# A four-layer image kernel: the column-wise copy of an image made by transfers in memory, after layer 0's merge, in place of copies on ScalarE during it

## The chip, the cores and the metric

The kernel runs on one core of a Trainium2 chip. The metric is the device time in microseconds (us). A run's time is a little longer than the span of its profile, which begins with the first recorded instruction and ends with the last. The engines are named as the profile names them: PE (TensorE), DVE (VectorE), ACT (ScalarE), POOL (GpSimd) and SP (SyncE, which here only issues transfers). All data is float32.

## What is computed

The input is two images of 128 channels and 128 x 128 pixels. Four layers follow each other, each of the form x + layer(groupnorm(x)): an axial attention along the columns (layer 0), a chain of four directional scans (layer 1), a deformable 3 x 3 convolution (layer 2), and a 4 x 4 convolution with stride 2 in transformed form (layer 3). The change lies between layers 0 and 1. Cut to what matters, layer 1 is:

```python
def _pass_once(x, w, vertical, reverse):
    if not vertical:
        x = jnp.transpose(x, (0, 1, 3, 2))
    if reverse:
        x = jnp.flip(x, axis=2)
    xs = jnp.moveaxis(x, 2, 0)
    def step(carry, xi):
        y = xi + jax.nn.relu(_conv1d(carry, w))      # 9 taps, 128 channels to 128
        return (y, y)
    _, ys = lax.scan(step, xs[0], xs[1:])
    ...
x = _pass_once(x, w_ud, vertical=True, reverse=False)
x = _pass_once(x, w_du, vertical=True, reverse=True)
x = _pass_once(x, w_lr, vertical=False, reverse=False)
x = _pass_once(x, w_rl, vertical=False, reverse=True)
...
x = x + _L1_conv_ref(_gn(x), ...)                    # the x that is added is layer 0's output
```

So the image that leaves layer 0 is needed twice: normalised, as the input of the scans, and untouched, to be added to their result. Two scans go through the rows and two through the columns; the last goes through the columns from right to left.

## The kernel before

**The tile `both`.** One tile of 128 partitions (channels) by 2 images by 128 rows by 128 columns, 128 KB in each partition, holds both images from the merge to the end (`res[n]` is image n). The four scans work in it in place, so layer 0's output is gone from it once layer 1 has normalised and scanned it.

**Layer 0** leaves its two parts in memory: `sv`, by column, and `sve`, by row. `Merge` (L889) puts them together in 16 half units: a unit is 32 columns of one image, a half unit 16. Units 0 to 3 are image 0, units 4 to 7 image 1. For each half unit `run` (L968) does this:

- `add` (L987), twice with 8 columns: ACT scales 8 columns of the sums `tv` into a tile `u` (L992), turning them to row order; DVE scales the part `te` and adds `u` to it (L1001). `u` has two buffers.
- `to_image` (L1003): POOL adds the upper 64 rows of `te` to the image, DVE the lower 64 (L1010); then DVE takes four pieces of group statistics, the lower rows first, so that the last two wait for POOL (L1012).
- `by_column` (L1016), one half unit late: ACT copies 8 columns of the finished image to a tile `bc` in column order and issues its store to the scratch tensor `x1_d` in memory, twice (L1021, L1023). `x1_d` is thus stored by column. `bc` has three buffers.

The loads of `te` (2 MB a unit), `tv` (1 MB a half unit) and the input image (1 MB for 16 rows) are issued on SP in a written order (`InOrder`, which also holds the order of the engines' instructions): a `te` two units ahead, a `tv` one unit ahead. `te` and `tv` have two buffers each, so a load waits until the buffer's last reader is done. All transfers of SP and ACT share eight semaphores in turn; one waits for the transfer before it on its semaphore, about eight back.

**Layer 1** (L1064) begins with the group norm's coefficients `gs` and `gb` (L1075), loads three more sets of scan weights on ACT's queue (L1058; POOL makes sums of them, L1060), and calls `layer3_weights` (L1694): it loads layer 3's weights `ta` on ACT's queue (L1706), POOL makes the transformed weights of it in 25 small instructions (L1713 to L1743), and the result `w3w` is stored to memory, again on ACT's queue (L1745), for layer 3 to read much later. Then come the scans.

A line of a scan is one row (or column) of both images. Its 9 taps are done in three groups of products with the even and odd pixels apart: 14 matmuls of 128 x 128 by 128 or 130 columns on PE (L1158). ACT copies the first product out as `c0` (L1168), DVE makes `v`, `u` and the new even and odd halves `new[0]`, `new[1]` and their sum `new[2]` (L1169 to L1175). These feed the next line's products, so a scan is one chain of dependent lines. In scans 0 to 2 ACT writes the new line back into `both` with two copies, `res<-ln` in the profile (L1178). In scan 0 ACT also normalises the rows in place, four ahead (L1105, L1128). The last scan doesn't write back by copy: POOL adds the new line and the saved column of layer 0's output into `both` (L1181). Those columns come from `x1_d` in blocks `x1t` of 8 columns (1 MB, three buffers), loaded on SP two blocks ahead (L1095, L1135).

Layer 2 and layer 3 follow; the change doesn't touch them except for where layer 3's weights come from in time.

Of the kernel before, what the change touches and what calls it, by code (L numbers as in the profile page):

```python
# [7 lines left out]
F32 = mybir.dt.float32  # L8
# [7 lines left out]
P = 128  # L16
N = 2
S = 128
RT = 4
NT = S // RT  # L20
WC = 32
# [867 lines left out]
class Merge:  # L889

    def __init__(self, env, x, mem, x1_d, ctx):
        self.env, self.x, self.mem, self.x1_d, self.ctx = env, x, mem, x1_d, ctx
        self.units = [(n, wc) for n in range(N) for wc in range(NC)]
        self.sums, self.embedded = {}, {}
        self.sync = InOrder(env.tc, env.nc.sync)
# [69 lines left out]
    def run(self, prm, res, mv, st_gn):  # L968
        nc, tc = self.env.nc, self.env.tc
        HWC, HS = WC // 2, S // 2  # L970
        act, dve, pool = (InOrder(tc, e) for e in (nc.scalar, nc.vector, nc.gpsimd))
        sp, units = self.sp, self.units
        with ExitStack() as ctx:
            cp = ctx.enter_context(tc.tile_pool(name="mg_c", bufs=1))
            pp = ctx.enter_context(tc.tile_pool(name="mg_ps", bufs=1, space=PSUM))
            for part in range(4):
                self.load_rows(res[0], 0, part)
            a, shift = self.scales(cp, pp, prm, mv)

            def there(at, hf):  # L980
                n, wc = units[at]
                lo = wc * WC + hf * HWC
                return res[n][:, :, lo : lo + HWC]

            HQ = HWC // 2

            def add(at, hf):  # L987

                tv = self.sums.pop((at, hf))
                for q in range(2):  # L990
                    u = sp.tile([P, S, HQ], F32, name="u", tag="u")
                    act.activation(  # L992
                        u.rearrange("p h w -> p w h"),
                        tv[:, q * HQ : (q + 1) * HQ],
                        AF.Identity,
                        bias=shift,
                        scale=a[:, 0:1],
                    )
                    lo = hf * HWC + q * HQ
                    te = self.embedded[at][:, :, lo : lo + HQ]  # L1000
                    dve.scalar_tensor_tensor(te, te, a[:, 1:2], u, ALU.mult, ALU.add)  # L1001

            def to_image(at, hf):  # L1003

                n, wc = units[at]
                te = self.embedded[at][:, :, hf * HWC : (hf + 1) * HWC]
                image = there(at, hf)
                for h, engine in ((0, pool), (HS, dve)):
                    here = image[:, h : h + HS, :]
                    engine.tensor_tensor(here, te[:, h : h + HS, :], here, ALU.add)  # L1010
                for b in (2, 3, 0, 1):
                    dve.bn_stats(  # L1012
                        st_gn[:, n, wc * NB + hf * 4 + b, :], image[:, b * 32 : (b + 1) * 32, :]
                    )

            def by_column(at, hf):  # L1016
                n, wc = units[at]
                image = there(at, hf)
                for q in range(2):
                    t = sp.tile([P, HQ, S], F32, name="bc", tag="bc", bufs=3)  # L1020
                    act.copy(t, image[:, :, q * HQ : (q + 1) * HQ].rearrange("p h w -> p w h"))  # L1021
                    lo = wc * WC + hf * HWC + q * HQ
                    act.dma_start(out=self.x1_d[:, n, lo : lo + HQ, :], in_=t)  # L1023

            last = None
            for at in range(len(units)):
                for hf in range(2):
                    if at > 0:  # L1030
                        add(at, hf)
                        if at + 1 < len(units):
                            self.load_sums(at + 1, hf)
                    elif hf == 0:
                        for k in range(2):
                            add(0, k)
                            self.load_sums(1, k)
                        self.load_rows(res[1], 1, 0)
                        self.load_rows(res[1], 1, 1)
                    if last is not None:  # L1040
                        by_column(*last)
                    last = at, hf
                    to_image(at, hf)
                if at + 2 < len(units):
                    self.load_embedded(at + 2)
                if at in (0, 1):
                    self.load_rows(res[1], 1, at + 2)
            by_column(*last)

# [9 lines left out]
    return wl, ws  # L1061


def layer1(env, prm, res, both, x1_d, st_gn, st_next, first, prepare):  # L1064

# [1 line left out]
    nc, tc = env.nc, env.tc  # L1069
    HS = S // 2  # L1070
    with ExitStack() as ctx:
        cp = ctx.enter_context(tc.tile_pool(name="l1c", bufs=1))
        sp = ctx.enter_context(tc.tile_pool(name="l1s", bufs=3))
        with tc.tile_pool(name="l1pn", bufs=1, space=PSUM) as pn:
# [1 line left out]
        pp = ctx.enter_context(tc.tile_pool(name="l1ps", bufs=2, space=PSUM))  # L1076
        weights = [first] + [scan_weights(env, prm, cp, d) for d in range(1, 4)]
        prepare()
        xp = ctx.enter_context(tc.tile_pool(name="l1x", bufs=3))


        lines = [
# [7 lines left out]
            InOrder(tc, e) for e in (nc.tensor, nc.vector, nc.scalar, nc.gpsimd)  # L1090
        )

        CB = 8

        def load_columns(w0):  # L1095
            t = xp.tile([P, N, CB, S], F32, name="x1t", tag="x1t")
            nc.sync.dma_start(out=t, in_=x1_d[:, :, w0 : w0 + CB, :])
            return t

        def stats(t, n):  # L1100
# [17 lines left out]
        for d in range(4):  # L1118
            steps = list(range(S)) if d % 2 == 0 else list(range(S - 1, -1, -1))
            wl, ws = weights[d]  # L1120
            if d == 3:
                columns = {w0: load_columns(w0) for w0 in (S - CB, S - 2 * CB)}
            for at, line in enumerate(steps):
# [7 lines left out]
                new = [t[:, :, 2 : 2 + HS] for t in now]  # L1131
                if d == 3:
                    w0 = line // CB * CB
                    if line == w0 + CB - 1 and w0 >= 2 * CB:
                        columns[w0 - 2 * CB] = load_columns(w0 - 2 * CB)  # L1135
                    add = [columns[w0][:, :, line - w0, k::2] for k in range(2)]
                if at == 0:
                    for k in range(2):
                        dve.tensor_copy(new[k], here[k])
# [554 lines left out]
def layer3_weights(env, prm, w3_d):  # L1694
# [5 lines left out]
    with tc.tile_pool(name="l3w", bufs=1) as wp:  # L1700
# [2 lines left out]
        tk = [wp.tile([P, 4, 2, H], F32, name=f"tk{k}", tag=f"tk{k}") for k in range(2)]  # L1703
        w3 = wp.tile([P, W3], F32, name="w3w", tag="w3w")
        ws, wt = layer3_views(w3)
        nc.scalar.dma_start(out=ta.rearrange("p u v o -> p (u v o)"), in_=prm["w3"])  # L1706
        pool = nc.gpsimd
        zero = wp.tile([P, 2 * P], F32, name="zero", tag="zero")
        pool.memset(zero, 0.0)
# [27 lines left out]
        for half in range(2):  # L1737
# [4 lines left out]
            if half == 1:  # L1742
                pool.tensor_tensor(to[2], y, x, sub)  # L1743
                less(to[3], x, y)
        nc.scalar.dma_start(out=w3_d, in_=w3)  # L1745


def layer3(env, prm, res, w3_d, st_gn, out):
# [173 lines left out]
@with_exitstack  # L1922
def program(ctx, tc, prm, out):
    nc = tc.nc
    x = prm["x"]
    cst = ctx.enter_context(tc.tile_pool(name="cst", bufs=1))
    dram = ctx.enter_context(tc.tile_pool(name="scratch", bufs=1, space=DRAM))
    env = Env(tc, cst, prm["cst"])
    st_gn = [
        cst.tile([P, N, NT, 6], F32, name=f"st_gn{k}", tag=f"st_gn{k}") for k in range(2)  # L1930
    ]
    mem = {
        "qa": dram.tile([P, N, NC, WC, S], F32, name="qa_d", tag="qa_d"),
        "qb": dram.tile([P, N, NC, 4, 4, 8, WC], F32, name="qb_d", tag="qb_d"),
        "v": dram.tile([NG, N, NC, S, WC, 16], F32, name="v_d", tag="v_d"),
        "sv": dram.tile([P, N, NC, WC, S], F32, name="sv_d", tag="sv_d"),
        "sve": dram.tile([P, N, NC, S, WC], F32, name="sve_d", tag="sve_d"),
    }
    w3_d = dram.tile([P, W3], F32, name="w3_d", tag="w3_d")
    x1_d = dram.tile([P, N, S, S], F32, name="x1_d", tag="x1_d")  # L1940
    mem["px"] = dram.tile([N, TP, TP, P], F32, name="px_d", tag="px_d")
    mem["off"] = dram.tile([N, NT, P, 4, 27], F32, name="off_d", tag="off_d")
    tables = [
        dram.tile([TE * TE, 512], F32, name=f"table{n}", tag=f"table{n}") for n in range(N)
    ]

    alphas = cst.tile([P, NG, 3], F32, name="alphas", tag="alphas")
    layer0_prepare(env, x, prm, mem, alphas)
    mv = cst.tile([P, NG, 2, 2], F32, name="mv_out", tag="mv_out")
    merging = ctx.enter_context(ExitStack())  # L1950
    merge = Merge(env, x, mem, x1_d, merging)
    layer0_attention(env, prm, mem, alphas, mv, merge.begin)

    rp = ctx.enter_context(tc.tile_pool(name="res", bufs=1))
    both = rp.tile([P, N, S, S], F32, name="res", tag="res")
    res = [both[:, n] for n in range(N)]
    with tc.tile_pool(name="l1w", bufs=1) as wp:
        first = scan_weights(env, prm, wp, 0)
        merge.run(prm, res, mv, st_gn[1])
        merging.close()  # L1960
        layer1(
            env,
            prm,
            res,
            both,
            x1_d,
            st_gn[1],
            st_gn[0],
            first,
            lambda: layer3_weights(env, prm, w3_d),  # L1970
        )
    layer2(env, prm, res, mem, tables, st_gn[0], st_gn[1])
    layer3(env, prm, res, w3_d, st_gn[1], out)
# [129 lines left out]
```

## Time and profile before

| what | value |
|---|---|
| three runs | 5618.76, 5618.18, 5607.35 us; median 5618.18 |
| the profiled execution: its own time | 5624.39 us |
| its span | 5622.6 us |
| mean granted clock of PE in it | 0.966 |
| PE busy, share of the span | 5229.8 us, 93% |
| DVE, ACT, POOL busy | 66%, 47%, 27% |
| first load of the merge's image issued | 1966.5 us |
| last statistics of the merge end | 2129.6 us |
| first scan's first product, about | 2166 us |
| POOL's first add of the fourth scan | 3376.9 us |
| transfers: bytes, mean rate | 404.21 MB, 72 GB/s |

How to read it. The profile's second part cuts the span into 40 slices of 140.6 us; a digit is the busy share of an engine in tenths. In the view of stretches, each engine has its busy time in the stretch and the number of its instructions; then follow the clock granted to PE, the mean busy share of the 16 DMA engines and what they moved. In the view of waits, a line says who waited for whom: total us, how often, longest. In the timeline each row is a start, a duration and an instruction, out<-in with shapes; what stands in brackets is the idle time before it and what ended it. Nearly all of this kernel's instructions carry line 81, since the helper `InOrder` issues them; one goes by the names of tiles. `pl` is a scan's product in PSUM, `ln` the line's halves, `res` the image in `both`, `x_d` the scratch tensor `x1_d`.

### The profile page before, as it was taken

Reading aid. Unit: us, or ns where it says so; the run is one execution under the profiler, and the core shown is the slowest. Engines: PE = TensorE matmul, PEld = TensorE weight load, DVE = VectorE, ACT = ScalarE, POOL = GpSimd, SP = SyncE. Lnnn points to the kernel's source line nnn. Section 1 sums busy time; section 2 is a strip of 40 time slices with the busy share of each in tenths; the row PEclk is TensorE's granted clock in tenths of the full one; section 3 lists DMA queues with packets and bytes.
Section 4 is the critical chain, followed back from the end, with each engine's and each line's share of the span. In section 5 each row is a group of like instructions: output and inputs, shape, how many; then the busy total and the mean of one; then the engine's idle time right before and its main releaser. Section 6 shows DMA issues by size and latency. Waiting matters only on the chain. (4 is left out here: it accounts for less than half of the span.)

```text
span 5622.6 us, 171669 instructions
## 1 busy us (share of the span) xinstructions
PE 5229.8 (93%) x71931; PEld 4656.8 (83%) x71931; DVE 3685.4 (66%) x7132; ACT 2652.3 (47%) x7896; POOL 1530.1 (27%) x1169
## 2 busy tenths in 40 slices
PE   8997999999999805999999999999799999999999
PEld 6866888888888605999999999994599998999877
DVE  3635888888888764555555556663466666666698
ACT  1056899898898774443223330003233333333322
POOL 2114666666666632000000003330000000000376
PEclk8998999999999957999999999999899999999999
DMA  3353333333333392000000001104567677766211
GB/s 151 107 219 84 60 60 61 62 62 61 60 61 60 94 396 89 1 1 2 1 1 1 1 1 39 39 25 121 105 88 88 88 83 85 91 88 87 47 50 57
DMA packets 413991, 404.21 MB, mean 72 GB/s; under 512 B 63520, under 2 KB 368544, under 8 KB 402336
## 3 DMA queue, kind: packets, MB, share of 16 engines
q1 hardware_dynamic: 404000, 365.18, 31.7%
q10 hardware_dynamic: 9216, 27.95, 1.3%
q8 instruction: 576, 9.44, 0.7%
q14 instruction: 199, 1.63, 0.1%
HBM read 252.31 MB, written 140.68 MB: 70 GB/s over the span
## 5 line engine op out<-in xcount | busy, mean ns | idle before, releaser
L81 PE MATMUL pl<-ln,wl 128*128 128x128 f32 (+1 forms) x10160 | 1239.6, 276 | 31.4 <-DVE ln L81 31.4
L81 PEld LDWEIGHTS pl<-ln,wl 128*128 128x128 f32 x10160 | 1176.3, 190 | 42.3 <-issue 28.0
L81 ACT ACTIVATE e<-e,mx 128x128 f32<-128x128 f32 x2048 | 798.4, 398 | 0.8 <-DVE mx L81 0.8
L81 ACT COPY sm<-ps_s 128x432 f32<-128x432 f32 (+1 forms) x768 | 319.0, 489 | 787.3 <-PE ps_s L81 787.3
L81 POOL TENSOR_TENSOR e<-e,total 128x1024 f32<-128x1024 f32 x256 | 485.6, 1897 | 477.6 <-DVE total L81 466.6
L81 ACT COPY res<-ln 128x128 f32<-128x128 f32 x762 | 263.3, 345 | 721.3 <-DVE ln L81 721.3
L81 PE MATMUL ps_s<-s,xw 100*128 100x144 f32 x4096 | 545.0, 286 | 0.1
L81 POOL TENSOR_TENSOR res<-ln,x1t 128x128 f32<-128x128 f32 x256 | 134.1, 524 | 1495.3 <-DVE ln L81 1495.3
L81 DVE COPY s<-ps_w 100x1152 f32<-100x1152 f32 x256 | 346.6, 1354 | 294.1 <-PE ps_w L81 293.9
L81 PE MATMUL po<-sm,wdef 128*128 128x256 f32 x2304 | 539.1, 379 | 0.0
L81 PE MATMUL pl<-ln,ws 128*128 128x128 f32 x4064 | 537.5, 274 | 0.0
L81 POOL COPY et<-et 128x1024 f32<-128x1024 f32 x256 | 516.4, 2017 | 33.1 <-DVE et L81 24.5
L81 PEld LDWEIGHTS ps_s<-s,xw 100*128 100x128 f32 x4096 | 517.0, 190 | 0.6 <-ACT sm L81 0.5
L81 DVE TENSOR_TENSOR v<-pl,c 128x128 f32<-128x128 f32 x508 | 148.2, 292 | 538.2 <-PE pl L81 538.2
L81 PEld LDWEIGHTS pl<-ln,ws 128*128 128x128 f32 x4064 | 495.3, 191 | 0.0
L81 ACT ACTIVATE r<-gen,alphas 128x1536 f32<-128x1536 f32 x256 | 395.4, 1544 | 169.2 <-PE gen L81 138.6
L81 PEld LDWEIGHTS po<-sm,wdef 128*128 128x128 f32 x2304 | 419.8, 190 | 47.7
L81 POOL MEMSET col<- 128x10 f32 (+1 forms) x72 | 6.0, 123 | 1483.2 <-DVE res L81 1475.6
L81 ACT ACTIVATION_READ_ACCUMULATOR e<-e,mx 128x1 f32 x2048 | 400.0, 195 | 0.0
L81 DVE SCALAR_TENSOR_TENSOR ln<-v,res 128x128 f32<-128x128 f32 x1016 | 343.7, 338 | 49.2 <-DVE v L81 1.2
L81 PE MATMUL te<-cst_main,e 128*128 128x128 f32 x2048 | 337.8, 287 | 27.1 <-POOL e L81 20.1
L81 DVE COPY et<-te 128x512 f32<-128x512 f32 x512 | 349.2, 682 | 13.4 <-PE te L81 12.6
(245 smaller groups left out, 9215.3 us busy)
## 6 DMA issues: line engine op xcount, KB each, us to landing
xw<-px_d SPq DMA_DIRECT2D x1280, 80.0 KB
xa<-in_x SPq DMA_DIRECT2D x16, 1024.0 KB
v_d<-vs SPq DMA_DIRECT2D x16, 1024.0 KB
qb_d<-sb SPq DMA_DIRECT2D x16, 1024.0 KB
qa_d<-sa SPq DMA_DIRECT2D x8, 2048.0 KB
zz<-qb_d SPq DMA_DIRECT2D x1024, 16.0 KB
vt<-v_d SPq DMA_DIRECT2D x64, 256.0 KB
qk<-qa_d SPq DMA_DIRECT2D x256, 64.0 KB
```

The lines of the kernel that those rows point to most:

```text
L81: return lambda *a, **k: self.tc.keep_in_program_order(issue(*a, **k))
```

## The change

It has four parts. By-column copies and their stores go from the merge (`by_column` and its calls), and `u` gets four buffers. At the start of layer 1, 17 transfers on SP store `both` to `x1_d` by row: rows 0 to 3, then 15 blocks of 8 rows, then rows 124 to 127. After `prepare()`, eight transfers on SP copy `x1_d` to a second scratch tensor `x1c_d` from memory to memory, the last block of columns first; `x1c_d` holds blocks of 16 columns, in each of which a partition's part is contiguous. One such transfer moves 32768 runs of 64 bytes, 2 MB. The fourth scan loads blocks of 16 columns (2 MB, two buffers, one block ahead), in which a column's elements lie 64 bytes apart. And `layer3_weights` issues its load and its store on SP in place of ACT. In the built program the load of `ta` stands behind the 17 row stores on SP, and the store of `w3w` behind the first of the eight copies and ahead of the other seven.

```diff
@@ Merge.run
-                    u = sp.tile([P, S, HQ], F32, name="u", tag="u")
+                    u = sp.tile([P, S, HQ], F32, name="u", tag="u", bufs=4)
...
-            def by_column(at, hf):
-                n, wc = units[at]
-                image = there(at, hf)
-                for q in range(2):
-                    t = sp.tile([P, HQ, S], F32, name="bc", tag="bc", bufs=3)
-                    act.copy(t, image[:, :, q * HQ : (q + 1) * HQ].rearrange("p h w -> p w h"))
-                    lo = wc * WC + hf * HWC + q * HQ
-                    act.dma_start(out=self.x1_d[:, n, lo : lo + HQ, :], in_=t)
...
-                    if last is not None:
-                        by_column(*last)
-                    last = at, hf
                     to_image(at, hf)
...
-            by_column(*last)
@@ layer1
     with ExitStack() as ctx:
+        for lo, hi in [(0, 4)] + [(h, h + 8) for h in range(4, S - 4, 8)] + [(S - 4, S)]:
+            nc.sync.dma_start(out=x1_d[:, :, lo:hi, :], in_=both[:, :, lo:hi, :])
...
         prepare()
-        xp = ctx.enter_context(tc.tile_pool(name="l1x", bufs=3))
+        xp = ctx.enter_context(tc.tile_pool(name="l1x", bufs=2))
...
-        CB = 8
+        CB = 16
+        for k in range(S // CB - 1, -1, -1):
+            nc.sync.dma_start(
+                out=x1c_d[k].rearrange("p n h w -> p (n h) w"),
+                in_=x1_d.rearrange("p n h w -> p (n h) w")[:, :, k * CB : (k + 1) * CB],
+            )
...
-            t = xp.tile([P, N, CB, S], F32, name="x1t", tag="x1t")
-            nc.sync.dma_start(out=t, in_=x1_d[:, :, w0 : w0 + CB, :])
+            t = xp.tile([P, N, S, CB], F32, name="x1t", tag="x1t")
+            nc.sync.dma_start(out=t, in_=x1c_d[w0 // CB])
...
-                    if line == w0 + CB - 1 and w0 >= 2 * CB:
-                        columns[w0 - 2 * CB] = load_columns(w0 - 2 * CB)
-                    add = [columns[w0][:, :, line - w0, k::2] for k in range(2)]
+                    if line == w0 + CB - 1 and CB <= w0 < S - CB:
+                        columns[w0 - CB] = load_columns(w0 - CB)
+                    add = [columns[w0][:, :, k::2, line - w0] for k in range(2)]
@@ layer3_weights
-        nc.scalar.dma_start(out=ta.rearrange("p u v o -> p (u v o)"), in_=prm["w3"])
+        nc.sync.dma_start(out=ta.rearrange("p u v o -> p (u v o)"), in_=prm["w3"])
...
-        nc.scalar.dma_start(out=w3_d, in_=w3)
+        nc.sync.dma_start(out=w3_d, in_=w3)
@@ program
+    x1c_d = dram.tile([8, P, N, S, 16], F32, name="x1c_d", tag="x1c_d")
```

More of the change, by code (lines that the diff above doesn't have):

```diff
@@ L889, with __init__ @@
 class Merge:
-    def __init__(self, env, x, mem, x1_d, ctx):
-        self.env, self.x, self.mem, self.x1_d, self.ctx = env, x, mem, x1_d, ctx
+    def __init__(self, env, x, mem, ctx):
+        self.env, self.x, self.mem, self.ctx = env, x, mem, ctx
         self.units = [(n, wc) for n in range(N) for wc in range(NC)]
@@ L1014, in to_image @@
                     )
-            def by_column(at, hf):
-                n, wc = units[at]
-                image = there(at, hf)
-                for q in range(2):
-                    t = sp.tile([P, HQ, S], F32, name="bc", tag="bc", bufs=3)
-                    act.copy(t, image[:, :, q * HQ : (q + 1) * HQ].rearrange("p h w -> p w h"))
-                    lo = wc * WC + hf * HWC + q * HQ
-                    act.dma_start(out=self.x1_d[:, n, lo : lo + HQ, :], in_=t)
-            last = None
             for at in range(len(units)):
@@ L1061, in scan_weights, with layer1 @@
     return wl, ws
-def layer1(env, prm, res, both, x1_d, st_gn, st_next, first, prepare):
+def layer1(env, prm, res, both, x1_d, x1c_d, st_gn, st_next, first, prepare):
     nc, tc = env.nc, env.tc
@@ L1950, in program @@
     merging = ctx.enter_context(ExitStack())
-    merge = Merge(env, x, mem, x1_d, merging)
+    merge = Merge(env, x, mem, merging)
     layer0_attention(env, prm, mem, alphas, mv, merge.begin)
@@ L1966, in program @@
             x1_d,
+            x1c_d,
             st_gn[1],
```

## The prediction, made before the changed kernel had run

> **What bounds the kernel now.** I read the busy slices first, to find the stage that the change touches, then the stretches of 20 us, the waits, and the timelines of DVE and ACT inside it.
>
> ```profile
> PE   8997999999999805999999999999799999999999
> ...
> DMA  3353333333333392000000001104567677766211
> ```
>
> One slice is 140.6 us. PE is the bound nearly everywhere; it stands still only in slices 14 and 15 (1968 to 2166 us), the merge that ends layer 0, while the DMA row shows its only 9. The change lives there and in the scans behind it. The stretches show two limits in turn:
>
> ```profile
> core 0: us, PE busy (x) PEld busy (x) DVE busy (x) ACT busy (x) POOL busy (x), PEclk, DMA share, GB/s
> ...
> 1980.00:2000.00 20.00, 0.00 (x0) 0.00 (x0) 9.48 (x12) 9.11 (x5) 3.67 (x2) 0.50 1.01 420
> ...
> 2080.00:2100.00 20.00, 0.00 (x0) 0.00 (x0) 15.19 (x16) 17.89 (x11) 8.01 (x3) 0.50 0.99 360
> ...
> 2140.00:2160.00 20.00, 0.00 (x0) 0.00 (x0) 0.94 (x2) 0.00 (x0) 16.49 (x23) 0.50 0.24 86
> ```
>
> Early the DMA engines are full (420 GB/s) and the engines half idle; later ACT leads (17.9 of 20); at the end POOL works alone, and neither DMA nor ACT moves. Who waits:
>
> ```profile
> DVE te L81 <- ACT u L81: 34.2, 32, 12.2
> ...
> ACT res L81 <- POOL w3w L1717: 24.7, 1, 24.7
> ...
> ACT u L81 <- DMA tv<-sv_d: 11.7, 2, 11.2
> ...
> DVE mv_l L54 <- DMA x_d<-bc: 6.0, 1, 6.0
> ```
>
> DVE waits for ACT; the group norm waits 6.0 us for the last store by column; the scan's first normalisation waits 24.7 us for layer 3's weights, because their store (L1745) is issued on ACT's queue ahead of it. One half unit on DVE:
>
> ```profile
> 2095.50 1.29 DVE L81 SCALAR_TENSOR_TENSOR te<-te,a_out,u 128x1024 f32<-128x1024 f32 x1 [0.54 <-ACT u L81]
> 2097.51 1.28 DVE L81 SCALAR_TENSOR_TENSOR te<-te,a_out,u 128x1024 f32<-128x1024 f32 x1 [0.72 <-ACT u L81]
> 2098.83 1.23 DVE L81 TENSOR_TENSOR res<-te,res 128x1024 f32<-128x1024 f32 x1
> 2100.09 1.29 DVE L81 BATCH_NORM_STATS2 st_gn<-res 128x6 f32<-128x512 f32 x2
> 2102.35 1.29 DVE L81 BATCH_NORM_STATS2 st_gn<-res 128x6 f32<-128x512 f32 x2 [0.98 <-POOL res L81]
> 2104.18 1.28 DVE L81 SCALAR_TENSOR_TENSOR te<-te,a_out,u 128x1024 f32<-128x1024 f32 x1 [0.54 <-ACT u L81]
> ```
>
> The beat is 8.68 us, of which 1.26 us is waiting for ACT. The merge's last statistics end at 2129.64, the group norm's coefficients at 2140.97, and DVE's first v of scan lines 1, 2 and 3 starts at 2170.16, 2174.16 and 2177.29; from there a line takes 3.13 us, with PE full.
>
> **What the Trainium skill says.** "DMA: Bandwidth & Descriptors", section "Where 436 GB/s comes from": a ceiling of 435 GB/s for all 16 engines. The trace agrees: 420 to 426 GB/s at share 1.0, and stores alone near 310 us reach 426 and 422. Same page, "Latency and other measured facts": rows at a pitch of 512 KiB fall to 207 GB/s. Here the image loads (pitch 64 KiB) run at 420, and the 4 KB packets of the by-column stores (pitch 128 KiB) take 159 ns each, 412 GB/s over 16 engines; no run here shows 512 KiB. Same page, "Measured (HBM→SBUF...)": about 10.5 ns per packet at the least. "SBUF — State Buffer", "Who interferes with whom": a DVE instruction with two SBUF inputs and a GpSimd one that reads SBUF exclude each other. The trace agrees: POOL's add takes 2407 ns with DVE idle and 3442 beside DVE's add of 1226.
>
> **The change, part by part.** Times are those of the profiled execution.
>
> (1) The copies by column go: 32 on ACT at 1898 ns, 60.7 us, and 32 stores' issues. Per half unit ACT keeps two activations, 4.2 us, and with four u buffers runs ahead. DVE's half unit then has no wait for ACT: first step 1.32, then from the second one's start to the last statistics (2097.51 to 2103.64) 6.13, in all 7.45. Its 0.98 us wait for POOL stays. DVE is next late.
>
> (2) But DVE must first get its data. Without the stores, loads run back to back at 2.46 us per MiB (426 GB/s) from the first image packet at 1967.5: image 0 (8 loads) to 1987, two sums to 1992, four loads of image 1 to 2002, te of unit 2 to 2007, two more to 2012, the sum that half (2,0) needs to 2014.2. About 1 us of landing and 2.3 of ACT later DVE starts (2,0) at 2017.5, against 2026.11 now. What follows needs 4 MiB per unit, 9.9 us, against 14.9 of DVE, so DVE leads to the end: 2017.5 + 0.7 + 12 × 7.45 = 2107.6, against 2129.64. The merge gains 22 us.
>
> (3) The bytes come back as 17 row stores on SP, all behind POOL's last add (1.3 us before that end, as at 2128.32 now): first packet at 2107.3. They are 3840 packets of 4 KB at 159 ns and 512 of 2 KB at 84, 653.6/16 = 40.9 us; the three scan weights on ACT's queue, 384 packets at 178 ns, share the engines: 4.3. With 1 us of landing all is stored at R = 2153.5. Eight semaphores allow some 7 stores in flight, about 17 us of work, so the issue doesn't starve the engines.
>
> (4) The new wait. In the built program the normalisations wait only for the store of their own rows; but ACT's first write-back of a scanned line (L1178, line 1, both images in one access) waits for all 17 stores. Behind it on ACT stand the next normalisations and the copy c0 of line 2; for c0 waits DVE, for DVE waits PE. So the scan does line 1, PE does line 2's products, and all stop until R. This takes the place of the 6.0 and the 24.7.
>
> (5) Layer 3's weights on SP: the load goes behind the 17 stores, its store no longer stands before the normalisation. The 24.7 us wait is gone from ACT; POOL's 17 us of weights (2146.98 to 2164.14), hidden by nothing today, run beside scan lines 3 to 8. The lock can hold a DVE step by up to 0.7 us; PE has about 0.7 us of other products per dependent step to cover that, so I take 1 us (0 to 5). On SP that store holds seven of the eight copies until POOL is done.
>
> (6) Copies in memory: 8 × 32768 packets of 64 bytes, 16384 per engine. The trace shows no copy from memory to memory. Below, 10.5 ns gives 172 us; above, the mean of the trace's 512-byte packets (57 ns) gives 934. I take 30 ns, 490 us. Needed at:
>
> ```profile
> 3376.86 0.96 POOL L81 TENSOR_TENSOR res<-ln,x1t 128x128 f32<-128x128 f32 x2 [1212.71 <-DVE ln L81]
> ```
>
> Three scans cover it: from about 2180 to 3361 less two loads (12 us) leaves 1169 us, 71 ns a packet. Both ends cost nothing; without cover it would be the whole 490. Instruction fetches use the same DMA engines; layer 2 runs PE at 9 tenths beside a DMA share of 6 or 7 tenths, so 0.5 us (0 to 10).
>
> (7) Fourth scan: 8 loads of 2 MB for 16 of 1 MB, each asked for 16 lines (52 us) ahead, 5 us long. POOL reads one operand at a stride of 128 bytes in place of 8; nearest row: DVE's step goes from 293 to 383 ns when its operand's stride grows. POOL's 0.47 and 0.58 in a 3.27 us line have room: 1 us (0 to 6).
>
> Sum: from R, two write-backs, two normalisations and c0 take 1.7 us on ACT, v and new[0] 0.6 on DVE; then PE, back at clock 0.5 after its rest, does nine products of line 3 in 4.9 instead of 2.5. v of line 3 starts at R + 7.2 = 2160.7, line 4 loses 0.7 more to the clock: 16.6 - 0.7 = 15.9 us ahead of 2177.29. Less 1 + 0.5 + 1 of (5) to (7), none of which can gain, since PE is full in these scans: a gain of 13.4 us. On the profiled execution's 5624.4 (span 5622.6 and 1.8 around it) that is 5611.0; this execution is 6.2 above the median of 5618.2, so I forecast 5605. Its own range, with 5 us on the stores and 3 on the merge, is 5596 to 5612.
>
> **The rivals.** A, the wait of (4) doesn't bind: then the first normalisation follows the group norm, at 2107.6 + 5.4 = 2113 for 2164.55, and 51 us go: 5567. For it: normalisations wait by rows. Against it: the built program's wait list. B, slower: the stores run at a pitch of 64 KiB on 256 rows at once, and writes don't keep 412 GB/s. At the skill's 207 they take 81 us for 41, R = 2194, and the time is 5645. From a loss of 13 us on the stores, below about 310 GB/s, nothing is left of the gain. Against it: 412 to 426 for stores in this trace. C, slower: the 64-byte copies take over 71 ns a packet; at 100 ns POOL gets its columns 470 us late, 6074. D, the gain is eaten: POOL's lock, fetches and strides at their upper ends (18.5 us more than taken): 5607 to 5623, about 5615.
>
> **How the numbers follow.** Forecast 0.60, D 0.20, B 0.08, C 0.07, A 0.05. About 0.2% (11 us) is what this measurement can tell from no change. Faster: 0.51 of the forecast, A, and 0.01 of D, 0.57; same: 0.09 and 0.17, 0.26; slower: B, C and 0.02 of D, 0.17. The range 5592 to 5628 takes in the forecast and D, leaving A, B and C out (0.20).
>
> **What would show it.** No wait of te for u from 2018 on and a half unit of 7.45; the merge's last statistics near 2108; ACT idle some 30 us before its first res<-ln, released by a DMA of x_d<-res near 2153; POOL's weights beside the scan; POOL not waiting for x1t at the fourth scan. It would be wrong if the scan runs through without that stop, if the stores end past 2165, or if a line of the first three scans takes over 3.2 us.

## The result, and the profile after

| | before | after |
|---|---|---|
| median of 20 runs each, us | 5614.38 (5607.35 to 5627.07) | 5603.71 (5598.65 to 5612.14) |
| the profiled execution's own time and span, us | 5624.39, 5622.6 | 5604.11, 5602.3 |
| mean granted clock of PE in it | 0.966 | 0.968 |

The ratio after to before is 0.9978, 95% interval 0.9972 to 0.9984: faster by 12.4 us (9.0 to 15.7). The ratio is estimated from all the single runs and is not the quotient of the two medians, which differ by 10.7 us. The forecast was 5605 and a gain of 13.4. The hit is partly luck: the base that it started from, the median of the three runs then known, lies 3.8 us above the median of 20, and some of its terms were off in opposite directions, as the steps below show.

The two traces differ by 20.3 us, and not all of that is the change. Layer 0, which is untouched, let the merge start 2.9 us earlier, and layers 2 and 3, untouched too, took 5.7 us less. What the change touches reaches from the issue of the merge's first image load (1966.46 before, 1963.53 after) to DVE's first instruction of layer 2's group norm (3795.19 and 3780.55). I call this the stage: 1828.7 us before, 1817.0 after, a gain of 11.7. Its two ends, in the kernel before and in the kernel after:

```profile
1966.46 4.03 SPq L81 DMA_DIRECT2D res<-in_x  x8
3795.19 1.84 DVE L54 BATCH_NORM_AGGREGATE mv_l<-st_gn 128x2 f32<-128x192 f32 x2
```

```profile
1963.53 3.96 SPq L81 DMA_DIRECT2D res<-in_x  x8
3780.55 1.84 DVE L54 BATCH_NORM_AGGREGATE mv_l<-st_gn 128x2 f32<-128x192 f32 x2
```

Below, times from the start of the stage are used where two executions are compared.

The busy slices of the kernel after, PE and DMA:

```profile
PE   8997999999999806999999999999799999999999
...
DMA  3353333333333379900000000104677777777211
```

The hole in PE is still there, one slice of 0 and then a 6 where a 5 was. In the merge's slice the DMA row fell from 9 to 7, and the two slices behind it, 2 and 0 before, are now 9 and 9: the stores by row and then the copies in memory. Stretches of the kernel after (columns as in the prediction's view):

```profile
core 0: us, PE busy (x) PEld busy (x) DVE busy (x) ACT busy (x) POOL busy (x), PEclk, DMA share, GB/s
1980.00:2000.00 20.00, 0.00 (x0) 0.00 (x0) 12.93 (x17) 8.23 (x4) 4.29 (x2) 0.50 1.03 427
2080.00:2100.00 20.00, 0.00 (x0) 0.00 (x0) 16.89 (x20) 8.27 (x4) 8.66 (x4) 0.50 0.28 117
2120.00:2140.00 20.00, 0.23 (x3) 0.04 (x1) 0.00 (x0) 0.00 (x0) 0.00 (x0) 0.64 1.02 421
```

From 2080 on ACT has 8.3 us of work in 20 where it had 17.9, DVE leads, and the memory is nearly idle. Then, from 2120 to 2140, hardly anything runs on the engines (PE 0.23 us of 20) while the memory runs at 421 GB/s. The waits of the kernel after, 1940 to 2185 us, say for what:

```profile
...
POOL tb L1721 <- DMA ta<-in_w: 40.4, 1, 40.4
DVE v L81 <- ACT c L81: 38.2, 2, 35.1
...
ACT res L81 <- DMA x_d<-res: 37.1, 3, 35.5
...
DVE te L81 <- ACT u L81: 14.0, 7, 8.3
```

The waits of ACT for `w3w` (24.7) and of `mv_l` for a store (6.0) are gone, and DVE's wait for `u` fell from 34.2 to 14.0, of which 8.3 is the one wait for data (for the sums that `u` is made of). In their place ACT waits 35.5 us for stores. One half unit on DVE, timeline of the kernel after:

```profile
2039.25 2.46 DVE L81 SCALAR_TENSOR_TENSOR te<-te,a_out,u 128x1024 f32<-128x1024 f32 x2
2041.75 1.23 DVE L81 TENSOR_TENSOR res<-te,res 128x1024 f32<-128x1024 f32 x1
2043.01 1.29 DVE L81 BATCH_NORM_STATS2 st_gn<-res 128x6 f32<-128x512 f32 x2
2045.27 1.28 DVE L81 BATCH_NORM_STATS2 st_gn<-res 128x6 f32<-128x512 f32 x2 [0.98 <-POOL res L81]
2046.48 2.46 DVE L81 SCALAR_TENSOR_TENSOR te<-te,a_out,u 128x1024 f32<-128x1024 f32 x2
```

7.23 us from one first step to the next, with only the wait for POOL left in it. And the stop, on ACT:

```profile
2110.32 3.18 ACT L81 ACTIVATE res<-res,gb_l,gs_l 128x128 f32<-128x128 f32 x8 [0.80 <-DMA x_d<-res]
2114.33 1.65 ACT L81 ACTIVATE res<-res,gb_l,gs_l 128x128 f32<-128x128 f32 x4 [0.82 <-DMA x_d<-res]
2115.89 0.24 ACT L81 COPY c<-pl 128x128 f32<-128x128 f32 x1
2151.64 0.50 ACT L81 COPY res<-ln 128x128 f32<-128x128 f32 x2 [35.50 <-DMA x_d<-res]
```

The normalisations of the first rows wait under 1 us for the stores of their own rows. The first write-back of a line waits until 2151.64, the time at which all 17 are stored. This is the prediction's R. The scan behind it, on DVE:

```profile
2158.52 0.29 DVE L81 TENSOR_TENSOR v<-pl,c 128x128 f32<-128x128 f32 x1 [3.56 <-PE pl L81]
2158.85 0.47 DVE L81 SCALAR_TENSOR_TENSOR ln<-v,res 128x128 f32<-128x128 f32 x1
...
2160.77 0.70 DVE L81 TENSOR_TENSOR ln<-ln,ln 128x128 f32<-128x128 f32 x1
2162.12 0.29 DVE L81 TENSOR_TENSOR v<-pl,c 128x128 f32<-128x128 f32 x1 [0.65 <-PE pl L81]
```

Line 3's `v` starts 6.9 us behind R. The next line takes 3.60 us and not 3.13: steps that took 0.29 us take 0.47 and 0.70 while POOL makes layer 3's weights (2155.72 to 2173.6). Where the gain arose and went, in us from the start of the stage:

| point | before | after | gain | predicted |
|---|---|---|---|---|
| merge's last statistics end | 163.2 | 140.9 | 22.3 | 22.0 |
| `v` of line 3 | 210.8 | 195.0 | 15.8 | 16.6 |
| POOL's first add of the fourth scan | 1410.4 | 1397.4 | 13.0 | 14.4 |
| layer 2's group norm | 1828.7 | 1817.0 | 11.7 | 13.4 |

(The predicted 14.4 is 16.6 less 0.7 for the clock, 1 for the lock, by which POOL and DVE exclude each other, and 0.5 for fetches.)

### The profile page after: what moved, and what is told of

Read it like the earlier page. It is cut to its first block, busy times and chain, and to the rows that moved or that the text cites. A ratio compares the mean times of both kernels' runs of the same rounds, so it can differ in the third digit from the quotient of the medians.

```text
span 5602.3 us, 171581 instructions
## 1 busy us (share of the span) xinstructions
PE 5231.9 (93%) x71931; PEld 4656.1 (83%) x71931; DVE 3690.4 (66%) x7132; ACT 2585.3 (46%) x7864; POOL 1546.2 (28%) x1169
## 5 line engine op out<-in xcount | busy, mean ns | idle before, releaser
L81 POOL TENSOR_TENSOR res<-ln,x1t 128x128 f32<-128x128 f32 x256 | 149.0, 582 | 1456.3 <-DVE ln L81 1456.3
L81 DVE SCALAR_TENSOR_TENSOR ln<-v,res 128x128 f32<-128x128 f32 x1016 | 346.3, 341 | 48.6 <-POOL res L81 0.9
```

Source lines behind the costliest of these rows:

```text
L81: return lambda *a, **k: self.tc.keep_in_program_order(issue(*a, **k))
```

## The experiments

The theory: the change buys 22 us in the merge and takes away the wait for layer 3's weights, and pays for both with one new stop, ACT's wait for the row stores, which ends last. The rivals: the stop is not what sets the time (something else would hold the scan as long), or the gain comes from the weights alone. "Against before" below is the median of 5 to 20 runs against that of the kernel before in the same set of runs (5614.4 to 5617.7 in the four sets). The ratio, with its 95% interval, is again estimated from the single runs, so the two columns differ by up to 2.5 us. "Stage" is the gain in the stage against before, from one trace each.

| kernel | median, us | against before | ratio | stage |
|---|---|---|---|---|
| after | 5603.71 | -10.7 | 0.9978 (0.9972 to 0.9984) | 11.7 |
| write-back by image | 5605.95 | -11.7 | 0.9978 (0.9968 to 0.9987) | 11.4 |
| before, weights moved | 5595.92 | -21.7 | 0.9959 (0.9945 to 0.9972) | 23.0 |
| after, weights not moved | 5606.45 | -11.2 | 0.9983 (0.9974 to 0.9993) | 7.7 |
| after, stores twice | 5649.35 | +31.7 | 1.0052 (1.0038 to 1.0066) | -29.2 |
| stores and write-back by image | 5573.40 | -43.4 | 0.9920 (0.9906 to 0.9933) | 48.0 |
| stores by image | 5591.06 | -25.8 | 0.9956 (0.9942 to 0.9969) | 21.0 |
| after, two `u` | 5603.39 | -13.4 | 0.9977 (0.9970 to 0.9984) | 12.5 |
| after, copies twice | 5604.24 | -12.6 | 0.9980 (0.9971 to 0.9989) | 12.3 |
| stores by image, image 0 first | 5577.14 | -38.9 | 0.9931 (0.9917 to 0.9944) | 42.2 |
| stores and write-back by image, again | 5570.32 | -45.7 | 0.9918 (0.9905 to 0.9932) | 46.9 |

**1. The write-back by image: a miss.**

```diff
-                        act.copy(here[k], new[k])
+                        if d == 0:
+                            for n in range(N):
+                                act.copy(both[:, n, line, k::2], new[k][:, n])
+                        else:
+                            act.copy(here[k], new[k])
```

> The kernel after, with the write-back of the first scan's lines made image by image: two ScalarE copies of 128x64 per line parity in place of one of 128x128, same values. Theory (the stall of 35 us at the first write-back is a wait for all 17 row stores that only the shape of the access brings, since one access over both images touches rows of every store): the wait goes, the scan runs on from the group norm at about 2110 us, and some 30 to 34 us of the stall are gained, less 1 to 2 us for four ScalarE copies per line in place of two: about 5572 us, 31 us under the kernel after. Rival (the stall is the memory's: the rows are needed in memory or the transfers hold the scan by themselves): the wait moves to another instruction and the time stays at 5604 within 3 us. Third way (ScalarE's doubled copies lengthen the 3.13 us line by more than 0.25 us): 128 lines take 32 us back, and the time is that of the kernel after although the stall is gone.

5605.95: nothing gained. ACT in this kernel:

```profile
2116.38 0.25 ACT L81 COPY res<-ln 128x64 f32<-128x64 f32 x1 [0.75 <-DVE ln L81]
2151.12 0.54 ACT L81 COPY res<-ln 128x64 f32<-128x64 f32 x3 [34.48 <-DMA x_d<-res]
```

The first copy, of image 0's row 1, no longer waits; the second, of image 1's row 1, waits as long as both did. The trace alone would fit the rival as well (a transfer that simply has to end), but it says where to look: the two differ only in the image. A store of rows lo to hi of both images reaches, in the tile, from row lo of image 0 to row hi of image 1. Image 1's row 1 lies within that stretch for all 17 stores, image 0's row 1 only for the first. In the built program the second copy does wait for all 17: the wait is one that the program asks for, whether or not the transfers still need that row. Not every access is held like this. The normalisations of image 1's rows lie within the same stretches and wait only for the store of their own rows, in the program and in the traces; they write a whole row without gaps, while a write-back writes every second element. No run writes back whole rows, so which accesses are held is known from these two kinds alone. So the stores' shape counts as well as the write-back's, and my expectation had looked at one side only. Experiments 5, 6 and 9 test this. The third way named there didn't happen: four small copies in place of two left the 3.13 us line alone.

**2. The weights alone.** The kernel before, with the two lines of layer 3's weights moved:

```diff
-        nc.scalar.dma_start(out=ta.rearrange("p u v o -> p (u v o)"), in_=prm["w3"])
+        nc.sync.dma_start(out=ta.rearrange("p u v o -> p (u v o)"), in_=prm["w3"])
...
-        nc.scalar.dma_start(out=w3_d, in_=w3)
+        nc.sync.dma_start(out=w3_d, in_=w3)
```

> The kernel before, with only the load and the store of layer 3's weights moved from ScalarE's queue to SyncE's; the copies by column stay. Theory (before, the first normalisation stood 24.7 us behind that store, so this small part alone would have given more than the whole change, whose stores by row then take the gain back): the normalisation follows the group norm at about 2141 us, 23 us are gained, less 2 for GpSimd's weights beside the scan: about 5593 us against 5614, and 10 us under the kernel after. Rival (the merge's copies are what counts and the weights' wait only covers another one, for the stores by column or for GpSimd): 5614 within 3 us.

5595.92, as the theory has it: these two lines alone give twice what the whole change gives. ACT in this kernel:

```profile
2139.29 0.20 ACT L45 ACTIVATE gs_l<-gs_l 128x2 f32<-128x2 f32 x1 [6.96 <-DVE gs_l L44]
2139.30 0.33 ACTq L1058 DMA_DIRECT2D wl<-in_wscan  x1
2139.97 4.72 ACT L81 ACTIVATE res<-res,gb_l,gs_l 128x128 f32<-128x128 f32 x12 [0.48 <-DVE gb_l L69]
```

The normalisation waits 0.48 us, for the group norm, where it waited 24.7 for POOL.

**3. The change without the weights' move.** The same two lines, back on ACT's queue.

> The kernel after, with layer 3's weights back on ScalarE's queue, so that only the copies by column are undone. Theory (the stall for the row stores ends last in any case and hides the wait for the weights, 2147 to 2164 before and some 22 us earlier now): the normalisation waits for the weights' store until about 2138, the first write-back for the row stores until about 2152, and the time is that of the kernel after, 5602 to 5606, a little less if GpSimd's weights no longer run beside the scan (2 us). Rival (the weights' move is what gave the gain): 5615 to 5625, no faster than before.

5606.45, half a us above the range expected, with an interval that overlaps that of the kernel after; in the stage it is 4.0 us worse. ACT:

```profile
2132.55 0.34 ACTq L1738 DMA_DIRECT2D w_d<-w3w  x1
2132.99 4.72 ACT L81 ACTIVATE res<-res,gb_l,gs_l 128x128 f32<-128x128 f32 x12 [25.77 <-POOL w3w L1710]
2137.62 0.24 ACT L81 COPY c<-pl 128x128 f32<-128x128 f32 x1
2155.14 0.50 ACT L81 COPY res<-ln 128x128 f32<-128x128 f32 x2 [17.28 <-DMA x_d<-res]
```

The wait of 25.8 us for the weights is back, and the next one, 17.3 us for the stores, ends last: the first is hidden under the second. So the weights' move, worth 21.7 us alone, is worth 0 to 4 in the change. What it has left is seen in two terms: with the weights' load (1 MB) and store (1.3 MB) among the row stores, all is stored 54.3 us after SP's first row store was issued, against 48.6; that is 5.7 us later, and 2.3 MB at 420 GB/s are 5.6. Against that, POOL's weights no longer run beside the scan: from R to the fourth scan it takes 1207.4 us against 1209.3, so the lock costs 1.9.

**4. Every row store twice.**

```diff
             nc.sync.dma_start(out=x1_d[:, :, lo:hi, :], in_=both[:, :, lo:hi, :])
+            nc.sync.dma_start(out=again_d[:, :, lo:hi, :], in_=both[:, :, lo:hi, :])
```

> The kernel after, with each of the 17 row stores issued twice, the second time into a scratch tensor that nobody reads: 33.6 MB in place of 16.8. Theory (the first write-back waits for the last store, and nothing hides that): its wait grows by one more time of the stores, 40.9 us at 412 GB/s, and the time to 5643 to 5646 us. Rival (the wait for the stores is covered, and the stop ends with something else, such as the scan's weights): unchanged within 5 us. If the stores run slower than 412 GB/s when they are many, the time is above 5650.

The stage grew by 40.9 us against the kernel after, as the theory has it. The median of 5649.35 lies above the 5643 to 5646 expected: the kernel before was 3.3 us slower in this set of runs than beside the kernel after, and against before the two kernels differ by 42.4 us (31.7 lost, 10.7 gained). ACT and two stretches of this kernel:

```profile
2192.96 0.50 ACT L81 COPY res<-ln 128x128 f32<-128x128 f32 x2 [73.41 <-DMA again_d<-res]
```

```profile
2110.00:2150.00 40.00, 8.62 (x56) 8.27 (x56) 2.32 (x9) 4.98 (x13) 2.52 (x2) 0.63 1.02 420
2150.00:2190.00 40.00, 0.00 (x0) 0.00 (x0) 0.00 (x0) 0.00 (x0) 0.00 (x0) 0.50 1.02 406
```

So each us of stores is a us of the kernel. With 406 to 420 GB/s the low rate that rival B feared doesn't come.

**5 and 6. The stores by image, with and without the write-back by image.**

```diff
-            nc.sync.dma_start(out=x1_d[:, :, lo:hi, :], in_=both[:, :, lo:hi, :])
+            for n in range(N):
+                nc.sync.dma_start(out=x1_d[:, n, lo:hi, :], in_=both[:, n, lo:hi, :])
```

Both, with the edit of the first experiment:

> The kernel after, with the write-back of the first scan's lines image by image as in the first experiment, and the 17 row stores made image by image as well (34 stores of 8 rows of one image). Theory (a strided access is held against the whole stretch from the first to the last row that a store reads; a store of both images stretches from image 0's rows to image 1's, so image 1's row 1 lies inside all 17, and only a store of one image sets it free): ACT's wait of 34.5 us is gone, the scan runs on from about 2116 us, held at most by the rows' own stores, and about 33 us go, less 2 for the lock with GpSimd's weights: 5570 to 5576 us, faster than both kernels and than the weights' move alone (5596). Rival 1 (the wait is for the transfers in any shape): 5604 within 4. Rival 2 (34 stores cost SyncE or the queue so much that the rows' own stores come late, and the normalisations wait): between 5580 and 5600.

5573.40, and 5570.32 when run again: 30 to 33 us under the kernel after (35 to 36 in the stage), 43 to 46 under before. ACT (the first of these two sets of runs):

```profile
2112.08 4.72 ACT L81 ACTIVATE res<-res,gb_l,gs_l 128x128 f32<-128x128 f32 x12 [0.43 <-DVE gb_l L69]
2116.71 0.24 ACT L81 COPY c<-pl 128x128 f32<-128x128 f32 x1
2118.38 0.40 ACT L81 COPY res<-ln 128x64 f32<-128x64 f32 x2 [1.43 <-DVE ln L81]
```

Here no wait for a store is left on ACT. And a stretch of the same kernel run again:

```profile
2120.00:2140.00 20.00, 19.89 (x179) 19.73 (x178) 10.26 (x37) 11.16 (x46) 0.00 (x0) 1.00 1.03 411
```

PE is full (19.9 of 20) at clock 1.00 beside the same stores at 411 GB/s, where in the kernel after it stood still. The stores take as long as ever; only nobody waits for them.

The stores by image alone:

> The kernel after, with only the row stores made image by image (34), the write-back left over both images. Theory (both sides' shapes count: the write-back over both images stretches from image 0's row 1 to image 1's, and so over all of image 0's later stores): the wait stays, 35 us at ACT, and the time is that of the kernel after, 5602 to 5608. Rival (the stores' shape alone brings the wait): 5570 to 5576.

5591.06: between the two expectations. The wait stays, as the theory has it, but is 27.8 us long and not 35:

```profile
2109.83 0.24 ACT L81 COPY c<-pl 128x128 f32<-128x128 f32 x1
2137.84 0.50 ACT L81 COPY res<-ln 128x128 f32<-128x128 f32 x2 [27.76 <-DMA x_d<-res]
```

What I had not thought of: image 0 is whole long before the merge ends, so a store of image 0 alone needn't wait for that end. Seven of them start early, beside the merge, in what was the memory's idle time:

```profile
2085.00:2095.00 10.00, 0.00 (x0) 0.00 (x0) 8.93 (x11) 2.53 (x2) 3.51 (x2) 0.50 0.53 218
```

218 GB/s, against 20 in the same stretch of the kernel after. From the end of POOL's last add to R it takes 39.5 us in place of 48.6: 9.1 of the 9.3 us that the stage gained.

**7. Two `u` buffers.**

```diff
-                    u = sp.tile([P, S, HQ], F32, name="u", tag="u", bufs=4)
+                    u = sp.tile([P, S, HQ], F32, name="u", tag="u")
```

> The kernel after, with two u buffers in place of four in the merge. Theory (without the copies ScalarE has 4.2 us of work in a half unit of 7.4, so DVE finds its u ready in any case): 5602 to 5607, the half unit unchanged. Rival (with two buffers ScalarE can't run ahead over a half unit, and DVE's wait of 0.5 to 0.7 us for u comes back in 12 to 16 half units): 6 to 11 us slower, 5610 to 5616.

5603.39, and half units of 7.24 us (2040.84 to 2048.08). The four buffers bring nothing here: ACT has 4.2 us of work in 7.2. The prediction gave them no time of their own, but spoke of them as the reason that ACT runs ahead; that reason isn't needed.

**8. Every copy in memory twice.**

```diff
+            nc.sync.dma_start(
+                out=again_d[k].rearrange("p n h w -> p (n h) w"),
+                in_=x1_d.rearrange("p n h w -> p (n h) w")[:, :, k * CB : (k + 1) * CB],
+            )
```

> The kernel after, with each of the eight copies from memory to memory issued twice, the second time into a scratch tensor that nobody reads: 33.6 MB in 64-byte pieces. Theory (the copies lie wholly beside three scans in which TensorE is full, and 210 us become 420, still 800 us ahead of the need): unchanged within 3 us, 5602 to 5608. Rival (they hold instruction fetches or the engines' own transfers, a cost that the kernel after already pays once): slower by as much as the first time cost, 3 to 10 us.

5604.24: nothing lost. SP's queue in this kernel, each issue waiting for a copy ahead of it to end:

```profile
2206.63 25.56 SPq L1087 DMA_DIRECT2D again_d<-x_d  x1
2232.24 25.54 SPq L1083 DMA_DIRECT2D x1c_d<-x_d  x1
2257.82 25.66 SPq L1087 DMA_DIRECT2D again_d<-x_d  x1
```

One copy takes 25.6 us, and moves 2048 packets of 64 bytes on each of 16 engines: 12.5 ns a packet. A stretch with copies in this kernel, and the same stretch of the kernel after, whose copies are done:

```profile
2380.00:2420.00 40.00, 39.89 (x358) 39.73 (x356) 20.86 (x76) 19.68 (x64) 0.00 (x0) 1.00 1.65 82
```

```profile
2380.00:2420.00 40.00, 39.89 (x357) 39.73 (x357) 20.98 (x76) 19.42 (x64) 0.00 (x0) 1.00 0.01 2
```

PE is busy for 39.89 of 40 us in both.

**9. All of image 0's stores ahead of image 1's**, the write-back as in the kernel after:

```diff
-        for lo, hi in [(0, 4)] + [(h, h + 8) for h in range(4, S - 4, 8)] + [(S - 4, S)]:
-            nc.sync.dma_start(out=x1_d[:, :, lo:hi, :], in_=both[:, :, lo:hi, :])
+        for n in range(N):
+            for lo, hi in [(0, 4)] + [(h, h + 8) for h in range(4, S - 4, 8)] + [(S - 4, S)]:
+                nc.sync.dma_start(out=x1_d[:, n, lo:hi, :], in_=both[:, n, lo:hi, :])
```

> The kernel after, with the row stores made image by image and all 17 of image 0 ahead of the 17 of image 1; the write-back is left as it was, over both images. Theory (the first write-back's stretch runs from image 0's row 1 to image 1's row 1, and so touches all of image 0's stores but of image 1's only the first; image 0 is whole long before the merge ends, and its 20 us of stores fit into the memory's idle time from about 2085 us on): the wait of 35 us at ACT is gone with no edit of the write-back, the scan runs on from about 2113 us, 5570 to 5576 us. Rival (the write-back waits for the last store whatever the order): 5588 to 5606. Third way (image 0's stores and the last loads or the merge hold each other): the merge's end moves by more than 2 us.

And beside it, on the same chip, the fastest kernel so far:

> The fastest kernel so far once more, beside the one with image 0's stores first on the same chip: 5570 to 5577 us. If image 0's early stores are worth anything beyond the wait (the 50 us in which scan and stores share the memory become 25), the other is faster by 1 to 3 us; if not, the two agree within 3, or the other is up to 1 us faster for its two ScalarE copies per line in place of four.

5577.14, 1 us above the range expected, with the wait of 35 us gone and no edit of the write-back. A write-back over both images reaches from image 0's row to image 1's, and so touches stores of image 0, which are early now, but of image 1 only those up to its own row. The trace shows one small price, on ACT:

```profile
2107.81 0.49 ACT L81 ACTIVATE res<-res,gb_l,gs_l 128x128 f32<-128x128 f32 x1 [1.18 <-DVE gb_l L69]
2112.74 4.34 ACT L81 ACTIVATE res<-res,gb_l,gs_l 128x128 f32<-128x128 f32 x11 [4.44 <-DMA x_d<-res]
```

Image 1's first row waits 4.4 us for its own store, which is now behind image 0's on SP. The stage is 4.7 us longer than that of the kernel beside it. Of the two ways to be rid of the wait, the one with both accesses by image is the faster by the traces and by 6.8 us between medians, though the intervals of the two ratios overlap (0.9905 to 0.9932 and 0.9917 to 0.9944). That is a miss for the expectation of the pair: it had image 0's early stores faster by 1 to 3 us, or the two within 3.

## Why the prediction was right, by its steps

(1) **The merge on DVE.** Taken 7.45 us a half unit, measured 7.23; behind the first half unit (2,0) the wait for `u` went but for one of 0.61 us, and the wait of 0.98 for POOL stayed, as written.

(2) **Data.** Half (2,0) started at 2016.03, in a trace whose stage began 2.9 us earlier: 1.5 us later than taken. That and the shorter half unit cancel: the merge gained 22.3 us, predicted 22.

(3) **The row stores.** R was taken as 2153.5; it was 2151.64, or 2154.6 on the clock of before. Doubling them cost 40.9 us, the same as the 40.9 worked out from packets of 159 and 84 ns. At the 64 KiB pitch of these stores the stretches shown have 406 to 421 GB/s, so rival B fell. Its price was also misread: the Trainium skill ("DMA: Bandwidth & Descriptors", section "Latency and other measured facts") has the 207 GB/s at a pitch of 512 KiB for copies between tensors in memory, and gives 214 as the full rate of the same copies. So 207 is almost full rate there, and not the fall to a half that the prediction took it for.

(4) **The new wait.** It was there, where it was put, and behind it stood what was named. Experiments 4 to 6 and 9 show that it alone holds the scan: rival A, whose premise was that this wait didn't bind, had 5567, and the kernels in which it doesn't came to 5570 and 5573. What was incomplete is its cause. "Both images in one access" was said of the write-back; it is as true of the stores. Curing the write-back alone gives nothing (experiment 1), and cutting the stores alone leaves a wait of 27.8 us (experiment 6) unless all of image 0's go first (experiment 9).

(5) **POOL's weights beside the scan.** Taken 1 us (0 to 5), 1.9 in experiment 3. The place was right: a DVE step that forms a sum of two SBUF operands takes 0.70 in place of 0.29 us beside POOL. Lines 3 to 7 take 3.4 to 3.6 us, over the 3.2 that the prediction had named as a sign of being wrong. That sign was set too tight: the third scan's lines take 3.21 in the kernel before already, and the excess ended with POOL's weights.

(6) **Copies in memory.** Taken 30 ns a packet on each engine, measured 12.5. The lower bound of 10.5 was misread. On the same page of the Trainium skill ("Measured (HBM→SBUF...)") it is 0.67 us over the 64 packets of one 4 KB transfer from memory to SBUF, and the prediction took it for each of 16 engines. Counted like that, over the whole transfer, a copy here takes 0.8 ns a packet (25.6 us over 32768), so the two numbers can't be set side by side. The cost was taken as 0, and a second set of copies costs nothing. The last of the eight is done near 2360 us, 1000 us ahead of POOL's first use, so rival C was never close. Whether the 0.5 us for fetches came, no run shows (see the sum).

(7) **The stride.** POOL's adds went from 0.47 and 0.58 us to 0.53 and 0.64; the fourth scan up to layer 2's group norm took 419.7 us for 418.3. Taken 1 us, measured 1.3. All ten traces with blocks of 16 columns have 419.6 to 419.9, both with blocks of 8 have 418.2 and 418.3; whether the stride or the larger loads cost it, no run tells apart.

**The sum.** Predicted 13.4, measured 11.7 in the stage and 10.7 between medians. Of the 1.7 us too much, 0.8 arose up to line 3 (R 1.1 later than taken, the way from R to line 3 0.3 shorter), 0.6 from there to the fourth scan, and 0.3 in it. The 0.6 is a balance: 2.8 us were lost there and 2.2 taken (0.7 clock, 1 lock, 0.5 fetches). The lock cost 1.9. The clock cost 0.1: in experiment 3, where no lock is in the way, line 3 takes 3.21 us and line 4 again 3.13. And 0.7 came from something that the prediction didn't have. In the kernel after, every 16th line of the first scan takes 3.48 us in place of 3.13, seven of them. PE pauses there, waiting for nothing that the profile shows, as its weight loads in one of these lines say:

```profile
2211.73 2.31 PEld L81 LDWEIGHTS pl<-ln,wl 128*128 128x128 f32 x20 [0.27 <-issue]
```

The kernel before has longer lines at the same spacing too, but in the second and third scan, 1.7 us in all against 2.4. The pauses are the same with the copies in memory doubled and go on after the copies are done, so it isn't the copies; their cause stays open. The part of rival D that came true is this: 4.1 us behind line 3, where 3.2 were taken.

**What the parts are worth** doesn't add up, and this is the core of the case. The weights alone give 21.7 us, the rest alone 11.2, both together 10.7. Once the stores by row stand in the way, the path to the scan ends with them whether the normalisation waited or not. Without that stop the two together give 43 to 46.

## What to carry to other kernels

When a change takes two waits off the path to one point and puts a third on it, ask of the third first what makes it wait: here it was only how the accesses on the two sides were cut, and cutting both by image was worth three times the change. A transfer whose result is needed much later should hold up nobody; look for the first instruction that overwrites what it reads, see how far each side's access reaches from its first to its last element and what the built program makes it wait for, and order or cut the transfers so that the early rows are free early. And try the smallest part of a change alone: two moved lines gave twice what the whole gave.

## What the runs showed of the hardware that was not expected

- A copy from memory to memory in 64-byte pieces ran at 12.5 ns a packet and engine, 82 GB/s as the profile counts it, with PE busy for 39.9 of 40 us beside it. I had taken 30 ns.
- With PE at full clock beside stores at 411 GB/s no loss is seen: 19.9 of 20 us busy.
- The same code before the stage started the merge at 1959.1 to 1966.5 us in the traces of the kernels, and the code behind the stage varied by up to 9 us as well (1819.2 to 1828.6). A single pair of traces (20.3 us apart here) would have shown the gain nearly twice too large; measuring from a fixed point to a fixed point gave 11.7.
